# A four-layer graph network on one core: the last norm, scaling and output by halves of the tokens for every graph, and a weight of 0.25 for 0.5 in the planner's order

## The chip, the core and the metric

The kernel runs on one core of a Trainium2 chip. A core has TensorE (PE, matrix products; PEld is its loading of the stationary operand), VectorE (DVE), ScalarE (ACT), GpSimd (POOL) and SyncE (SP), which here issues all DMAs. Each engine works through its own instructions in the order in which the program holds them and waits on semaphores for the others. The metric is the device time of one launch in microseconds.

## The reference

There are 32 graphs of N = 512 nodes with D = 256 features, each with an adjacency matrix of 512 x 512, all float32. Four layers follow each other, each with a residual and a layer norm without weights:

```python
def _layernorm(x, eps=1e-5): return (x - mean(x)) / sqrt(var(x) + eps)      # over the features
# layer 0: h = (1+eps)*x + adj@x;  f = relu(h@W1 + b1)@W2 + b2             (256 -> 512 -> 256)
# layer 1: h = adj@(x@W.T + b);    f = h where h > 0 else alpha*h
# layer 2: h = layer_norm(x)*gamma + beta;  f = x + relu((adj@h)@W_rel + b_rel + h@W_root)
# layer 3: h = (eps*x + adj@x)@W1 + b1;  f = silu(rmsnorm(h)*w)@W2 + b2    (256 -> 1024 -> 256)
# after each: x = _layernorm(x + f(x, adj))
```

Graphs don't depend on each other.

## The kernel before, in words

The tokens of a graph lie on 128 partitions, four to a partition (NC = 4 chunks); a "half" is two of the four chunks (HC = 2). Every matrix product is split into two by two blocks and made from seven block products, m1 to m7 (`seven`, line 651), with sums of the left and right blocks made ahead on DVE (`left_sums`, `right_sums`, `dense_sums`). Of a layer's products, `aggregate` is the one with the adjacency, `dense_feat` gives a result with features on partitions, and `dense_add` (line 850) adds its result into the residual: its `take` and `put` are DVE additions from PSUM, and it calls `done(j)` when half j of the tokens is complete. The three PSUM banks that `seven` uses are each filled anew after their additions were made.

The code does not issue instructions as it runs. It records operations (class `Op`) with the tiles that they read and write, and the class `Plan` then puts all of them, of all graphs, in one order, with prices of its own for each engine. At most FLIGHT = 5 graphs are under way at once; tiles come from pools (36 rooms for whole tensors, 11 small ones, 8 PSUM banks), and the planner picks which. Where an operation can run on ACT or DVE, it also picks the engine. An operation's rank is its graph's number times `period`, plus a need (`needs`, line 324): the matmul work of its graph that stands before the first matmul that depends on it, less the way there. For all but matmuls, the need is raised by `near` times the work between the operation and the next matmul that it feeds (capped at 20), so that a higher `near` lets an operation far from a matmul yield more:

```python
return [t if "tensor" in op.ways else t + near * b for op, t, b in zip(self.ops, need, between)]
...
rule = min(RULES, key=lambda rule: self.order(*rule)[0])   # (period, pace, last, near)
```

`last` is the period used for the last three graphs. Of the rules in RULES, the one whose order is the shortest by the planner's own prices is used. Where a two-operand DVE operation would hold up a power on POOL that is just about to start, the planner lets DVE pause; a pause is filled with `memset`s of a tile named `pause` (line 1197).

All instructions of the plan carry line 298 in the profile, and all DMAs of the plan line 316, so they are told apart by tiles: `room` is a whole tensor, `few` a small one, `ps` a PSUM bank, `A` and `L_gnn_W` are weights and their sums, `scrap` is the unused output of ACT's sums.

A layer norm is the class `Norm` (line 896). `half(h)` sums the values and their squared distances from the mean on ACT, per chunk, as soon as half h is complete. Then, in the graphs 0 to 30 after layer 3, `scales` makes the four chunks' scales at once: a `tensor_scalar` on DVE (128x4) and a power of -1/2 on POOL (128x4); `scaled` multiplies out the shift on DVE and applies scale and shift to the four chunks, on ACT or DVE (`put`); and one DMA of 512 KB stores the graph. Only the last graph uses `finish(h, ...)`, which does the same for two chunks: a 128x2 `tensor_scalar`, a 128x2 power, a 128x2 multiplication, two chunks scaled, one DMA of 256 KB. In graph 0 and graph 31 the class `NormOnVector` makes the sums on DVE instead.

SP issues, for each graph and in the order of the plan: the adjacency in four parts and x, the diagonals of two block sums out to memory and back, the layer-2 transposes as 16 small copies from room to room, a line with layer 3's scales out and back to all partitions, and the store.

Of the kernel before, what the change touches and what calls it, by code (L numbers as in the profile page):

```python
# [16 lines left out]
LN_EPS = 1e-5  # L17
# [74 lines left out]

RULES = [(42, 2, 10, 0.5), (42, 2, 16, 0.5)]


class Pool:
# [122 lines left out]
class Plan:  # L221
# [126 lines left out]
    def best(self):  # L348


        rule = min(RULES, key=lambda rule: self.order(*rule)[0])
        return self.order(*rule)[1]
# [109 lines left out]
def tile_gnn_stack(ctx: ExitStack, tc: tile.TileContext, a: dict, out: bass.AP):  # L462
# [26 lines left out]
    B, N, D = a["x"].shape  # L489
# [15 lines left out]
    plan = Plan(nc, FLIGHT)  # L505
# [9 lines left out]
    def alone():  # L515

        return plan.graph in (0, B - 1)
# [19 lines left out]
    def mm(o, lhsT, rhs, first, last):  # L537
        kw = dict(start=first, stop=last, skip_group_check=True)
        way = "tensor", "matmul", matmul_time(rhs.shape[-1]), (lhsT, rhs), kw
        plan.do(o, way, ordered=o.room)  # L540
# [4 lines left out]
    def act(o, x, func, **kw):  # L545
        plan.do(o, scalar(func, span(o), x, **kw))
# [7 lines left out]
    def add(o, x, y):  # L554
        plan.do(o, vector("tensor_add", span(o), x, y))
# [4 lines left out]
    def mul(o, x, y):  # L560
        plan.do(o, vector("tensor_mul", span(o), x, y))
# [20 lines left out]
    def room(*shape):  # L582
        return Part(Room(rooms)).shaped(*shape)

    def short(*shape):
        return Part(Room(rooms, whole=False)).shaped(*shape)
# [4 lines left out]
    def bank(*shape):  # L591
        return Part(Room(banks)).shaped(*shape)
# [4 lines left out]
    def half(t, h):  # L597
        return t[:, h * HC : (h + 1) * HC]
# [52 lines left out]
    def seven(x, y, z, product, take, put):  # L651


        product("m1", x, True)
        take(x, 0, 0)
        product("m5", z, True)
        take(z, 1, 1)
        product("m2", y, True)
        put(y, 0, 0, True)
        product("m6", x, False)  # L660
        take(x, 0, 1)
        product("m3", z, False)
        put(z, 0, 1, True)
        product("m7", x, False)
        put(x, 1, 1, True)
        product("m4", x, False)
        put(x, 1, 0, False)
# [29 lines left out]
    def blocks_of(*halves):  # L697

        return (W[:, :, i * P : (i + 1) * P] for i in range(2) for W in halves)
# [67 lines left out]
    def aggregate(x, adjacency):  # L767

        aT = room(DC, N)
        blocks = [  # L770
            x[:, j * HC : (j + 1) * HC, k * P : (k + 1) * P] for j in range(2) for k in range(2)
        ]
        t = room(4, HC, P)
        right = right_sums(*blocks, [t[:, i] for i in range(3)], t[:, 3])

        def product(m, ps, first):
            for k in range(HC):
                mm(ps, right[m][:, k, :], adjacency.left[m][:, k, :], first and k == 0, k == HC - 1)

        def block(i, k):  # L780
            return aT[:, k, i * TH : (i + 1) * TH]

        def take(ps, i, k):
            copy(block(i, k), ps)

        def put(ps, i, k, more):
            if more:
                add(block(i, k), ps, block(i, k))
            else:
                take(ps, i, k)  # L790

        seven(*(bank(TH) for _ in range(3)), product, take, put)
        return aT
# [13 lines left out]
    def dense_feat(aT, left, bias, hT, done):  # L807


        n = hT.n // 2  # L810
        t = room(3, TH)
        blocks = [aT[:, k, j * TH : (j + 1) * TH] for k in range(2) for j in range(2)]
        right = right_sums(*blocks, [t[:, i, :] for i in range(3)], blocks[1])
        for f0 in range(0, n, 2):

            def product(m, ps, first):
                for i in range(2):
                    w = left[m][:, (f0 + i) * P : (f0 + i + 1) * P]
                    mm(ps[:, i, :], w, right[m], first and i == 0, True)

            def block(i, j):
                return hT.pair(i * n + f0)[:, :, j * TH : (j + 1) * TH]

            def take(ps, i, j):
                for e in range(2):
                    f = i * n + f0 + e
                    act(block(i, j)[:, e], ps[:, e, :], AF.Identity, bias=bias[:, f : f + 1])

            def put(ps, i, j, more):
                if more:  # L830
                    add(block(i, j), ps, block(i, j))
                else:
                    take(ps, i, j)
                if i != j:
                    done(i * n + f0)

            seven(*(bank(2, TH) for _ in range(3)), product, take, put)
# [12 lines left out]
    def dense_add(x, right, left, done):  # L850


        def block(i, j):
            return x[:, j * HC : (j + 1) * HC, i * P : (i + 1) * P]

        def product(m, ps, first):
            n = len(right[m])
            for k in range(n):
                for i in range(HC):
                    mm(  # L860
                        ps[:, i, :], right[m][k][:, i * P : (i + 1) * P], left[m][:, k, :],
                        first and i == 0 and k == 0, k == n - 1,
                    )

        def take(ps, i, j):
            add(block(i, j), ps, block(i, j))

        def put(ps, i, j, more):
            take(ps, i, j)
            if i == 1:  # L870
                done(j)

        seven(*(bank(HC, P) for _ in range(3)), product, take, put)
# [123 lines left out]
    def everywhere(sums, ops):  # L997

        if alone():
            few = small(2, NC)  # L1000
            ve, power = few[:, 0, :], few[:, 1, :]
            by_token(ve, sums, *ops)
            inv_sqrt(power, ve)
            o = bank(N)
            for c in range(NC):
                flip(o[:, c * P : (c + 1) * P], power[:, c : c + 1].spread(P, P))
        else:
            few, turned = small(2, Q), small(Q)[0:Q]
            ve, square = few[0:Q, 0, 0 : N // Q], few[0:Q, 1, :]
            ts(ve, sums, *ops)  # L1010
            inv_sqrt(square[:, 0 : N // Q], ve)
            plan.do(turned, vector("transpose", Q, square))
            o, line = short(N), next(lines)
            name = line.tensor.name
            plan.move(line.rearrange("(m i) -> m i", i=Q), turned[0 : N // Q], N / 256, into=name)
            plan.move(o, line.partition_broadcast(P), P * N / 256, late=0.8, outof=[name])
        return o

    def plus_row(x, r):

        for h in range(2):
            add(half(x, h), half(x, h), r.unsqueeze(1).to_broadcast([P, HC, D]))
# [77 lines left out]
    def layer3(x, adjacency, b):  # L1100

        aT = aggregate(x, adjacency)
        plus_row(x, b2_3)
        hT, acc = Wide(FC3), short(N)

        def squares(f):
            sq = room(2, N)
            act(sq, hT.pair(f), AF.Square)
            if f == 0:
                add(acc, sq[:, 0, :], sq[:, 1, :])  # L1110
            else:
                add(acc, acc, sq[:, 0, :])
                add(acc, acc, sq[:, 1, :])

        dense_feat(aT, A1_3, b1_3, hT, squares)
        pr = everywhere(column_sums(acc), (1.0 / HID3, RMS_EPS, ALU.mult, ALU.add))
        right = {}
        for q in range(0, FH, 2):
            for f in (q, q + 1, FH + q, FH + q + 1):
                mul(hT.chunk(f), hT.chunk(f), pr)  # L1120
                act(hT.chunk(f), hT.chunk(f), AF.Silu, scale=w_3[:, f : f + 1])
            for m, t in dense_sums([hT.pair(q)], [hT.pair(FH + q)]).items():
                right[m] = right.get(m, []) + t
        norm = (NormOnVector if alone() else Norm)(x)
        place = out[b].rearrange("(p c) d -> p c d", c=NC)
        if b < B - 1:
            dense_add(x, right, A2_3, norm.half)
            norm.scales((1.0, LN_EPS))
            y = norm.scaled()
            plan.move(place, y, N * D / 256, into=f"out{b}")  # L1130
        else:

            def done(h):
                norm.half(h)
                norm.finish(h, 1.0, LN_EPS, half(place, h))

            dense_add(x, right, A2_3, done)

# [11 lines left out]
    x = load_x(0)  # L1152
# [12 lines left out]
    x = layer0(x, adjacency)  # L1165
# [9 lines left out]
    h = layer1(x, adjacency)  # L1175
# [9 lines left out]
    A2_3 = weight_sums("A2_3", *blocks_of(W2_3[:, 0:FH], W2_3[:, FH:]))  # L1185
    layer3(layer2(*h, adjacency), adjacency, 0)
    for b in range(1, B):
        plan.graph = b
        x, adjacency = load_x(b), Adjacency(b)
        h = layer1(layer0(x, adjacency), adjacency)  # L1190
# [45 lines left out]
```

## Time and profile before

| | |
|---|---|
| median of 3 runs | 2318.61 us (2318.61 to 2320.24) |
| profiled execution, its own time | 2319.3 us |
| its span, first to last instruction | 2317.5 us, at a granted TensorE clock of 0.999 |
| PE matmul / weight load busy | 2295.5 us (99%) / 2089.9 us (90%) |
| DVE / ACT / POOL busy | 2120.0 us (91%) / 1642.6 us (71%) / 256.9 us (11%) |
| chain that ended last | PE 89%, DVE 7%, ACT 2% |
| stores of 512 KB, 256 KB | 31 of 3.2 us, 2 of 2.4 us to landing (median) |

One record of a 128x256 or 128x128 float32 matmul is half of an instruction: each such product has two records. The span is the time that the profiler saw instructions; the execution's own time has 1.8 us more around it. A share of busy time is an average over start, steady state and end, so the stretches have to be read one by one. In the table of stretches, a count in parentheses is the number of instructions that are in the stretch.

### The profile page before, as it was taken

Reading aid. Unit: us, or ns where it says so; the run is one execution under the profiler, and the core shown is the slowest. Engines: PE = TensorE matmul, PEld = TensorE weight load, DVE = VectorE, ACT = ScalarE, POOL = GpSimd, SP = SyncE. Lnnn points to the kernel's source line nnn. Section 1 sums busy time; section 2 is a strip of 40 time slices with the busy share of each in tenths; the row PEclk is TensorE's granted clock in tenths of the full one; section 3 lists DMA queues with packets and bytes.
Section 4 is the critical chain, followed back from the end, with each engine's and each line's share of the span. In section 5 each row is a group of like instructions: output and inputs, shape, how many; then the busy total and the mean of one; then the engine's idle time right before and its main releaser. Section 6 shows DMA issues by size and latency. Waiting matters only on the chain.

```text
span 2317.5 us, 41158 instructions
## 1 busy us (share of the span) xinstructions
PE 2295.5 (99%) x14002; PEld 2089.9 (90%) x14002; DVE 2120.0 (91%) x5428; ACT 1642.6 (71%) x4444; POOL 256.9 (11%) x167
## 2 busy tenths in 40 slices
PE   9999999999999999999999999999999999999998
PEld 7889899999999999999999999999999999998988
DVE  8989999999899999999999999989999899989897
ACT  4676677776776776777767776767677677676776
POOL 0000001101101101011011111010110101101110
PEclk9999999999999999999999999999999999999999
DMA  7001222112221122211222211222112222201101
GB/s 241 21 18 19 62 58 60 24 55 62 58 60 28 54 59 65 55 43 41 56 65 57 60 25 56 61 58 59 38 46 58 65 55 52 78 13 24 55 15 42
DMA packets 223746, 122.83 MB, mean 53 GB/s; under 512 B 142896, under 2 KB 194352, under 8 KB 223536
## 3 DMA queue, kind: packets, MB, share of 16 engines
q1 hardware_dynamic: 223536, 120.20, 19.1%
q8 instruction: 111, 1.82, 0.3%
q14 instruction: 99, 0.81, 0.1%
HBM read 78.92 MB, written 24.97 MB: 45 GB/s over the span
## 4 chain that ended last, share of the span: by engine, by line
PE 89%; DVE 7%; ACT 2%; DMA 1%; issue 1%; SPq 0%; POOL 0%; ACTq 0%; DVEq 0%
PE ps L298 89%; DVE room L298 6%; ACT room L298 1%; ACT scrap L298 1%; DVE few L298 1%; DMA room<-in_x_dram 1%; DMA L_gnn_W<-in_L_gnn_W_dram 0%; DMA room<-in_adj_dram 0%; DMA L_gnn_b<-in_L_gnn_b_dram 0%; DMA diagonal<-room 0%; SPq L316 0%; ACT L298 0%; DVE A L298 0%; DVE L_gnn_W_root L298 0%; POOL few L298 0%
## 5 line engine op out<-in xcount | busy, mean ns | idle before, releaser
L298 PE MATMUL ps<-room,room 128*128 128x256 f32 x3584 | 930.9, 381 | 5.7 <-DVE room L298 3.2
L298 DVE TENSOR_TENSOR room<-room,room 128x512 f32<-128x512 f32 (+1 forms) x1360 | 773.0, 590 | 5.4 <-ACT room L298 2.8
L298 DVE TENSOR_TENSOR room<-ps,room 128x256 f32<-128x256 f32 (+1 forms) x1344 | 605.6, 469 | 143.7 <-PE ps L298 136.4
L298 PEld LDWEIGHTS ps<-room,room 128*128 128x128 f32 x3584 | 617.3, 191 | 70.3 <-DVE room L298 7.1
L298 PE MATMUL ps<-L_gnn_W,room 128*128 128x128 f32 (+1 forms) x3584 | 544.3, 290 | 1.9 <-DVE room L298 1.0
L298 PEld LDWEIGHTS ps<-L_gnn_W,room 128*128 128x128 f32 x3584 | 505.6, 191 | 33.7 <-ACT room L298 1.9
L298 PEld LDWEIGHTS ps<-A,room 128*128 128x128 f32 x3072 | 460.5, 191 | 47.3 <-DVE room L298 14.1
L298 PE MATMUL ps<-A,room 128*128 128x128 f32 x3072 | 486.9, 276 | 0.9 <-DVE room L298 0.7
L298 POOL TENSOR_TENSOR few<-few,mhalf 128x4 f32<-128x4 f32 (+2 forms) x161 | 256.2, 1598 | 2054.5 <-DVE few L298 1883.1
L298 ACT ACTIVATE room<-room,few 128x256 f32<-128x256 f32 x627 | 335.0, 596 | 159.9 <-DVE few L298 159.7
L298 PE MATMUL ps<-room,L_gnn_W 128*128 128x256 f32 x1536 | 416.4, 380 | 0.6 <-DVE room L298 0.5
L298 ACT ACTIVATE room<-ps,L_gnn_b_c 128x256 f32<-128x256 f32 x768 | 311.0, 476 | 122.3 <-PE ps L298 117.9
L298 DVE TENSOR_TENSOR room<-room 128x256 f32<-128x256 f32 (+1 forms) x640 | 308.7, 492 | 13.9 <-ACT room L298 8.2
L298 PE MATMUL ps<-room,A 128*128 128x256 f32 x1152 | 320.0, 380 | 1.1 <-ACT room L298 0.8
L298 ACT ACTIVATE room<-room 128x1024 f32<-128x1024 f32 (+2 forms) x260 | 240.8, 939 | 87.3 <-DVE room L298 84.4
L298 PEld LDWEIGHTS ps<-room,L_gnn_W 128*128 128x128 f32 x1536 | 274.5, 191 | 30.1 <-DVE room L298 1.9
L298 ACT ACTIVATE room<-ps 128x256 f32<-128x256 f32 (+1 forms) x513 | 180.1, 373 | 153.3 <-PE ps L298 153.1
L298 ACT ACTIVATE scrap<-room,few 128x256 f32<-128x256 f32 x504 | 250.7, 499 | 39.0 <-DVE few L298 38.3
L298 ACT ACTIVATE scrap<-room 128x256 f32<-128x256 f32 x504 | 206.7, 411 | 88.3 <-DVE room L298 79.8
L298 PEld LDWEIGHTS ps<-room,A 128*128 128x128 f32 x1152 | 202.8, 191 | 22.8 <-ACT room L298 2.0
L298 ACT ACTIVATE room<-room,L_gnn_rms_weight_c 128x512 f32<-128x512 f32 x256 | 173.2, 712 | 13.1 <-DVE room L298 11.0
L298 DVE TENSOR_TENSOR room<-room,loop 128x256 f32<-128x256 f32 x256 | 101.1, 411 | 2.9 <-DMA diagonal<-room 1.8
(57 smaller groups left out, 1110.6 us busy)
## 6 DMA issues: line engine op xcount, KB each, us to landing
room<-in_adj_dram SPq DMA_DIRECT2D x128, 256.0 KB, 5.0
room<-in_x_dram SPq DMA_DIRECT2D x31, 512.0 KB, 5.9
out_dram<-room SPq DMA_DIRECT2D x31, 512.0 KB, 3.2
room<-room SPq DMA_DIRECT2D x480, 32.0 KB, 2.0
diagonal<-room SPq DMA_DIRECT2D x62, 128.0 KB, 1.8
room<-in_adj_dram SPq DMA_DIRECT2D x124, 64.0 KB, 1.9
room<-diagonal SPq DMA_DIRECT2D x62, 128.0 KB, 2.2
room<-line SPq DMA_DIRECT2D x30, 256.0 KB, 3.3
```

The source lines that it names most:

```text
L298: getattr(getattr(self.nc, engine), method)(to, *(put(x) for x in args), **kw)
```

## The change

Every graph now uses the path that only the last one had: when half j of the last product is complete, `done` sums that half, and `finish` makes its two scales, scales its two chunks and stores them. The planner has one rule in place of two, with `near` at 0.25 in place of 0.5.

```diff
-RULES = [(42, 2, 10, 0.5), (42, 2, 16, 0.5)]
+RULES = [(42, 2, 10, 0.25)]
...
         norm = (NormOnVector if alone() else Norm)(x)
         place = out[b].rearrange("(p c) d -> p c d", c=NC)
-        if b < B - 1:
-            dense_add(x, right, A2_3, norm.half)
-            norm.scales((1.0, LN_EPS))
-            y = norm.scaled()
-            plan.move(place, y, N * D / 256, into=f"out{b}")
-        else:
-
-            def done(h):
-                norm.half(h)
-                norm.finish(h, 1.0, LN_EPS, half(place, h))
-
-            dense_add(x, right, A2_3, done)
+
+        def done(h):
+            norm.half(h)
+            norm.finish(h, 1.0, LN_EPS, half(place, h))
+
+        dense_add(x, right, A2_3, done)
```

Since all operations are ordered together, both edits can move any instruction of any engine.

## The prediction

> **What bounds the kernel now.** I read the page first: span, then the share of each engine.
>
> ```profile
> span 2317.5 us, 41158 instructions
> ...
> PE 2295.5 (99%) x14002; PEld 2089.9 (90%) x14002; DVE 2120.0 (91%) x5428; ACT 1642.6 (71%) x4444; POOL 256.9 (11%) x167
> ```
>
> PE has no matmul under way for 2317.5 - 2295.5 = 22 us. Where those lie is read from the table of stretches (columns: stretch, length, then busy us of PE, PEld, DVE, ACT, POOL, the clock, DMA share, GB/s):
>
> ```profile
> 0.00:103.00 103.00, 94.98 (x503) 81.72 (x504) 94.72 (x266) 53.87 (x154) 4.95 (x10) 1.00 0.47 145
> 103.00:277.00 174.00, 171.52 (x1029) 154.37 (x1029) 158.57 (x408) 120.10 (x306) 14.69 (x12) 1.00 0.14 32
> 277.00:1966.00 1689.00, 1688.84 (x10333) 1542.48 (x10332) 1553.16 (x3949) 1221.78 (x3331) 197.66 (x120) 1.00 0.20 52
> 1966.00:2309.00 343.00, 340.13 (x2142) 311.37 (x2140) 310.74 (x797) 242.70 (x647) 37.83 (x25) 1.00 0.13 36
> 2309.00:2317.50 8.50, 0.00 (x0) 0.00 (x0) 2.86 (x13) 4.14 (x11) 1.72 (x3) 0.66 0.47 185
> ```
>
> The idle time is 8.0 us at the start, 2.5 us while the flight of graphs fills, 0.2 us in 1689 us of steady work, 2.9 us while it runs out, and 8.5 us after the last matmul. PE bounds nearly all of it.
>
> "Busy" can hide matmuls that are spaced out, so I count. The groups by form give, per graph, 212 records of 128x256 and 224 of 128x128. In the timeline, a run of four of the first from 101.43 lasts 1.03 us, (1.03 - 0.38)/3 = 0.216 us each after the first (a lone one takes 0.38); a run of twenty of the second from 2297.74 lasts 2.40, (2.40 - 0.28)/19 = 0.112. The floor is 212 x 0.216 + 224 x 0.112 = 70.9 us; the load of x recurs every 71.2 us. About 0.3 us a graph is lost, about 7 us over some 24 steady graphs. One part shows at one place in the timeline (start, length, engine, work):
>
> ```profile
> 1066.06 0.14 DVE L298 TENSOR_TENSOR few<-few 128x4 f32<-128x4 f32 x1
> ...
> 1066.14 0.41 DVE L298 TENSOR_TENSOR room<-ps,room 128x256 f32<-128x256 f32 x1
> ...
> 1066.59 0.52 PEld L298 LDWEIGHTS ps<-A,room 128*128 128x128 f32 x4 [0.33 <-DVE room L298]
> ```
>
> In layer 2's last product the weight load waits for a DVE addition; the matmul comes 0.53 us after the one before, where 0.43 is its pace: 0.1 us, once a graph. DVE is late there because it is full for most of a graph:
>
> ```profile
> 992.60:1032.60 40.00, 40.00 (x239) 36.08 (x237) 39.71 (x109) 32.02 (x90) 5.38 (x4) 1.00 0.10 26
> 1032.60:1046.60 14.00, 14.00 (x78) 12.66 (x77) 8.72 (x16) 8.39 (x17) 0.00 (x0) 1.00 0.63 172
> 1046.60:1063.80 17.20, 17.20 (x126) 16.33 (x124) 16.98 (x44) 11.05 (x37) 2.89 (x1) 1.00 0.06 17
> ```
>
> Of one graph's 71.2 us DVE rests 5.8, nearly all of it in one stretch of 14 us. Outside that stretch, added DVE work has no room of its own: it is paid out of how far DVE runs ahead of PE.
>
> **What the skill says.** The Trainium skill, Perfetto Trace Analysis, "Identifying the Most-Contended Engine", says that matmul busy time does not tell the distance to the limit and that weight-load busy time does; the trace agrees (99% against 90%), hence the count of records above. The same skill, SBUF — State Buffer, "SBUF: two separate sides", says that GpSimd and VectorE take a shared port pair exclusively, and a blocked one waits for a whole instruction. The trace does not show it: beside the 2.89 us power on POOL from 1058.68, DVE additions with two SBUF operands take 0.40 to 0.41 us, their usual time. So I price no blocking for the added powers. DMA: Bandwidth & Descriptors, "Latency and other measured facts", puts a fixed cost of about 2 us on a DMA, so a half isn't half as long; the trace agrees (median 3.2 us to landing for 512 KB out, 2.4 for 256 KB).
>
> **The change, part by part.** *Rules.* The instruction order of the kernel before is that of rule (42, 2, 10, 0.5) alone; dropping the second rule changes nothing. *near from 0.5 to 0.25* adds no operation and reorders. *Halves* add, in each of 31 graphs, one TENSOR_SCALAR and one TENSOR_TENSOR of 128x2 on DVE, one power on POOL, one DMA issue on SP. The engines' orders also hold 157 pauses (memsets on DVE ahead of an operation that must let a power through) where 72 were: in 24 graphs there are 5 where there was 1, before a layer-3 product `mul`, because the PSUM addition that stood between the layer-2 scale and it has moved. Prices, from the groups of instructions (count, then busy us and mean ns of one, then the idle time before):
>
> ```profile
> L298 POOL TENSOR_TENSOR few<-few,mhalf 128x4 f32<-128x4 f32 x97 | 116.7, 1204 | 716.6 <-DVE few L298 635.1 <-DVE pause L1197 48.9 <-ACT scrap L298 29.7
> ...
> L1197 DVE MEMSET pause<- 128x48 f32 x72 | 7.1, 98 | 2.5
> ...
> L298 POOL TENSOR_TENSOR few<-few,mhalf 128x2 f32<-128x2 f32 x2 | 1.4, 696 | 2.6 <-DVE few L298 2.6
> ```
>
> POOL: 2 x 0.70 for 1.20, +0.2 us a graph on an engine 89% idle: free. SP: one more issue, 0.54 us; each DMA waits for its half's scaling, and behind it in SP's queue stand layer 2's transposes and the loads of the next graph (4 of adj, one of x). The first half's store stands ahead of the transposes, the second in the old place just ahead of the loads, which are used a graph later; I price it at 0, covered by that lead. If the early store were held up, the transposes and then layer 2's last product would be late. ACT does the same scalings, 4 a graph. DVE: two small ops at a pace of about 0.07 (a pair of such ops takes 0.22, one 0.16) and 4 memsets of 0.098: 0.14 + 0.39 = 0.53 us a graph, and the memsets stand in the full stretch.
>
> *Steady state.* In both orders PE's matmuls repeat graph after graph; beside the matmuls of other work, few operations of a graph have moved by over 3 us. At the place of the 0.1 us stall, the work on PE between layer 2's second product and the late matmul was two 128x256 and eight 128x128 matmuls (2 x 0.43 + 8 x 0.224 = 2.65 us); now three and eight, 3.08 us, for a DVE sequence that is a transpose shorter. The stall should go: -0.1. A new tight place is layer 0's first dense product on its first difference: four wide and four narrow matmuls, 2.6 us, cover an addition, two 128x512 transposes and a subtraction, 0.34 + 2 x 0.63 + 0.41 plus 0.26 for three hand-overs = 2.27 us; 0.35 us is left at best where 1.4 us stood, and less if DVE arrives late. What the 0.53 us cost PE isn't shown before. Bounds: -0.3 a graph (all waiting gone) and +0.53 (no cover). I take -0.05, since the stall goes and some of the lead is spent: 24 x -0.05 = -1.2 us.
>
> *Start and run-out.* All engines' orders are the same up to ACT's operation at 101.5 us; PE's first difference is its 257th matmul, at 103.25. So the 8.0 us stays. From there to 277 and from 1966 the orders differ; 5.4 us of idle is at stake and is dealt anew: I take 0, bounds -3 and +4.
>
> *Tail.* The chain of waits ends not in graph 31 but in graph 30: four scalings of graph 29, its own totals, its scale, a power, then scalings.
>
> ```profile
> 2306.95 2.07 ACT room L298 x4
> ...
> 2310.29 1.02 POOL few L298
> ```
>
> By halves, graph 29's scalings come before PE ends, and half of graph 30's. The power is 0.70 for 1.02, one or two 0.49 us scalings leave the end. Graph 31's own chain, unchanged, is next late; its last scaling would end about 1 us before the old end. Last stores are 2 x 256 KB for 512 + 256. I take -1.2, bounds -2 and 0.
>
> **Sum** against the profiled execution (2319.3; span 2317.5 and 1.8 around it): -1.2 - 1.2 = -2.4, so 2316.9; the median shown is 2318.61, 0.7 lower, hence 2316.2. A measurement of this kernel tells about 0.2% from no change, 4.6 us.
>
> **Rivals.** *No change to speak of, 2316.2*: for it, the shared order and PE's floor. Chance 0.55. *Faster, 2311*: half of the 0.3 us a graph (24 x -0.15 = -3.6), -2 at run-in and run-out, -1.7 in the tail: -7.3. For it: the stall has cover now, and halves free rooms sooner; against: most of the loss isn't at one place that the change touches. Chance 0.27. *Slower, 2330 at its full price*: DVE becomes the bound in its full stretch. The 5 memsets before the layer-3 product, and the two small operations, go straight to PE's next waiting matmul: 24 x 0.53 = +12.7 beside the tail's -1.2. Half of it gives 2324. It decides once PE's cover behind the pause is used up; from 0.24 us a graph on (+5.8) it shows as slower. For it: DVE at 39.71 of 40 us; against: the reordering moved covers too. Chance 0.18, a third of it above 2327. That the edit does nothing is excluded by the orders.
>
> **How the numbers follow.** The likeliest case alone spans 2314 to 2323. The range goes on to both others: 2309, where a fifth of the faster case is left out, and 2327; that leaves out about 0.05 + 0.06.
>
> **What would show it.** Right: PE's idle time in 277 to 1966 stays under 2 us, loads of x recur within 0.1 us of 71.2, the weight-load wait on the layer-2 addition is gone, the last stretch is 7 to 8 us, memsets 157. Wrong: PE waiting on DVE in every graph behind the 5 memsets or at layer 0's dense product, a period of 71.4 or more, or SP's loads landing late.

## The result, and the profile after

The changed kernel takes 2342.5 us (median of 4 runs, 2340.91 to 2342.85) beside 2319.43 us for the kernel before in the same session: a ratio of 1.0098, interval 1.0086 to 1.011, 23 us slower. It lies outside the predicted range of 2309 to 2327. The profiled span is 2340.7 us.

The head of the page, with the shares by engine, hides it:

```profile
span 2340.7 us, 41411 instructions
...
PE 2307.0 (99%) x14002; PEld 2087.4 (89%) x14002; DVE 2142.8 (92%) x5574; ACT 1650.4 (71%) x4445; POOL 261.2 (11%) x198
```

The shares have moved by a point at most. The chain that ended last, by engine, has moved from PE 89%, DVE 7% to:

```profile
DVE 53%; PE 36%; issue 5%; ACT 4%; DMA 1%; DVEq 0%; SPq 0%; ACTq 0%; POOLq 0%; POOL 0%
```

The table of stretches (columns as in the prediction) says where:

```profile
0.00:103.00 103.00, 94.74 (x502) 81.51 (x502) 94.10 (x264) 53.23 (x152) 4.37 (x9) 1.00 0.47 145
103.00:277.00 174.00, 172.48 (x1052) 158.23 (x1052) 162.19 (x419) 123.96 (x322) 20.90 (x14) 1.00 0.14 32
277.00:1966.00 1689.00, 1677.07 (x10192) 1516.23 (x10191) 1551.88 (x4022) 1211.37 (x3277) 192.59 (x140) 1.00 0.19 51
1966.00:2332.00 366.00, 362.30 (x2260) 331.20 (x2260) 331.77 (x859) 258.04 (x687) 41.58 (x33) 1.00 0.14 39
2332.00:2340.70 8.70, 0.37 (x4) 0.18 (x2) 2.84 (x14) 3.81 (x10) 1.81 (x3) 0.72 0.36 136
```

PE's idle time in 277 to 1966 is 1689.00 - 1677.07 = 11.9 us, where it was 0.2; the other stretches are within 1 us of before. Idle time is not all. I add, for every PE record, its distance from the one before less the pace of its kind (0.2165 us for 128x256, which the prediction rounds to 0.216, and 0.112 for 128x128). This pacing loss was 16.8, 5.0 and 5.9 us before (up to 280, 280 to 1950, after 1950) and is now 13.6, 30.6 and 7.0. So steady work loses 25.6 us more, the start 3.2 less and the run-out 1.1 more. The mean period of a graph is 72.3 us, where it was 71.2.

The list of waits in 300 to 1950 (engine waiting, its releaser: us in total, times, longest) names the places:

```profile
PEld ps L298 <- DVE room L298: 31.0, 69, 0.9
...
DVE few L298 <- POOL few L298: 18.6, 23, 0.8
...
PE ps L298 <- DVE room L298: 11.9, 23, 0.5
PEld ps L298 <- ACT room L298: 11.4, 47, 0.3
```

The third line is new, with one wait in each of 23 graphs; before, no such wait was in this window, and the first line stood at 11.9 us. The fourth is new too, but for one wait of 0.3 us: two weight loads a graph now wait for ACT. The timeline shows the place, the same in every graph, about 72.3 us apart:

```profile
1034.50 1.30 DVE L298 STREAM_TRANSPOSE room<-room 128x512 f32<-128x512 f32 x2
1034.61 1.03 PE L298 MATMUL ps<-room,A 128*128 128x256 f32 x4
...
1035.71 0.38 DVE L298 TENSOR_TENSOR room<-room 128x256 f32<-128x256 f32 x1
...
1036.15 0.70 PE L298 MATMUL ps<-room,L_gnn_W 128*128 128x256 f32 x2 [0.52 <-DVE room L298]
```

Two transposes, a subtraction, then layer 0's first dense product on the difference: the "new tight place" of the prediction. The matmul comes 0.68 us later than PE's pace would have it. In this graph (981.2 to 1053.8) PE records are late by 1.47 us in all, if each that is late by over 0.03 us is counted: 0.78 at this product, 0.40 around the two weight loads that wait for ACT, 0.29 elsewhere. A graph of the kernel before has 0.39. The pauses are the other thing to see, in DVE's timeline (start, length, work):

```profile
1015.97 0.15 DVE L298 TENSOR_SCALAR few<-few 128x4 f32<-128x4 f32 x1
1016.07 0.80 DVE L1191 MEMSET pause<- 128x48 f32 x5
1016.78 0.64 DVE L298 TENSOR_TENSOR room<-room,room 128x512 f32<-128x512 f32 x1
```

Five memsets of 98 ns each hold DVE from 1016.07 until the next operation starts at 1016.78, 0.71 us: they start about 0.175 us apart. In the kernel before, the one memset at this place holds DVE for 0.03 us:

```profile
1008.86 0.10 DVE L1197 MEMSET pause<- 128x48 f32 x1
1008.89 0.63 DVE L298 TENSOR_TENSOR room<-room,room 128x512 f32<-128x512 f32 x1
```

### The profile page after: what moved, and what is told of

It reads as the page before. It is cut to its first block, busy times and chain, and to the rows that moved or that the text cites. A ratio compares the mean times of both kernels' runs of the same rounds, so it can differ in the third digit from the quotient of the medians.

```text
span 2340.7 us, 41411 instructions
## 1 busy us (share of the span) xinstructions
PE 2307.0 (99%) x14002; PEld 2087.4 (89%) x14002; DVE 2142.8 (92%) x5574; ACT 1650.4 (71%) x4445; POOL 261.2 (11%) x198
## 4 chain that ended last, share of the span: by engine, by line
DVE 53%; PE 36%; issue 5%; ACT 4%; DMA 1%; DVEq 0%; SPq 0%; ACTq 0%; POOLq 0%; POOL 0%
DVE room L298 48%; PE ps L298 36%; DVE few L298 5%; ACT scrap L298 3%; DMA room<-in_x_dram 1%; DVE pause L1191 0%; ACT room L298 0%; DMA L_gnn_W<-in_L_gnn_W_dram 0%; DMA room<-in_adj_dram 0%; DMA L_gnn_b_rel<-in_L_gnn_b_rel_dram 0%; DVEq L298 0%; SPq L316 0%; DVE A L298 0%; DVE L_gnn_W L298 0%; POOLq L1226 0%
## 5 line engine op out<-in xcount | busy, mean ns | idle before, releaser
L298 PE MATMUL ps<-room,room 128*128 128x256 f32 x3584 | 917.8, 382 | 6.5 <-DVE room L298 3.4
L298 PEld LDWEIGHTS ps<-A,room 128*128 128x128 f32 x3072 | 455.6, 191 | 43.3 <-DVE room L298 12.0
L298 POOL TENSOR_TENSOR few<-few,mhalf 128x2 f32<-128x2 f32 (+3 forms) x192 | 260.5, 1362 | 2074.3 <-DVE few L298 1682.6
L298 PE MATMUL ps<-A,room 128*128 128x128 f32 x3072 | 481.1, 276 | 0.8 <-DVE room L298 0.7
L298 ACT ACTIVATE room<-room,L_gnn_rms_weight_c 128x512 f32<-128x512 f32 x256 | 178.2, 713 | 23.0 <-DVE room L298 22.9
```

Source lines behind the costliest of these rows:

```text
L298: getattr(getattr(self.nc, engine), method)(to, *(put(x) for x in args), **kw)
```

## The experiments

Medians in us and ratios to the kernel before, with 95% intervals. "Added" is the difference of medians to the kernel before measured in the same session (2319.21 to 2319.80). Experiments without pauses replace the loop of memsets by `pass`; the order of all else stays.

**e1: `near` alone.** In the kernel before:

```diff
-RULES = [(42, 2, 10, 0.5), (42, 2, 16, 0.5)]
+RULES = [(42, 2, 10, 0.25)]
```

> The kernel before with the one rule (42, 2, 10, 0.25): no halves. Its order holds 4 memsets ahead of layer 3's product in 25 graphs, where before has 1. A, the memsets in DVE's full stretch decide: in the kernel after, 5 memsets hold DVE 0.72 us a graph where 1 held it 0.03; 4 should hold it about 0.55, so +0.5 x 24 = +12, 2331 us. B, near moves layer 0's subtraction behind the two transposes and that alone decides: as slow as after, 2340. C, the halves' own operations and DVE's wait for the half's power (0.81 us a graph) decide: no change, 2319.

2326.93, 1.0034 [1.0021, 1.0047]: added 7.7, which lies between the expected cases. The steady period is 71.4 and the steady loss 9.7 (5.0 before), the loss after 1950 12.8 (5.9 before). The layer-0 wait isn't there.

**e2: halves alone.** The changed kernel with its `near` back at 0.5:

```diff
-RULES = [(42, 2, 10, 0.25)]
+RULES = [(42, 2, 10, 0.5)]
```

> The kernel after with the rule (42, 2, 10, 0.5) of before: halves, but near as before. Its order has 1 memset ahead of layer 3's product as before and 2 ahead of a column sum's addition in 24 graphs. A: the 2 memsets cost about 0.2 us and the two small pairs of operations 0.25 + 0.2 us of DVE: half of it uncovered, +5, 2324 us; at most +0.65 x 24 = +16. B: no change, 2319. C: nearly all of the loss, 2337 to 2342.

2338.18, 1.0082 [1.0067, 1.0097]: added 19.0. That is the number of case C, but not for its reason: the steady loss is 8.4 only, and the loss after 1950 is 20.9. Two PE waits of its run-out in the timeline:

```profile
2088.59 1.20 PE L298 MATMUL ps<-A,room 128*128 128x128 f32 x8 [3.82 <-DVE room L298]
...
2295.74 0.70 PE L298 MATMUL ps<-room,L_gnn_W 128*128 128x256 f32 x2 [2.23 <-DVE room L298]
```

Behind the first of them the granted TensorE clock is lower for some 7 us (the clock is the number ahead of the last two), while it is 1.00 at this place in the kernels before and after:

```profile
2088.00:2092.00 4.00, 2.90 (x16) 2.67 (x16) 1.98 (x7) 2.05 (x7) 0.70 (x1) 0.70 0.39 135
2092.00:2096.00 4.00, 3.23 (x11) 2.58 (x11) 3.84 (x7) 3.46 (x7) 0.00 (x0) 0.50 0.50 141
```

With 0.95 from 2096 to 2100, this is worth at most about 3.4 us of the 15 that this run-out loses more than before (an estimate from the three clocks). So the effects don't add up: each edit alone gives an order of its own, and the layer-0 stall belongs to the joint order only.

**e3: the changed kernel without pauses.**

```diff
             if op.pause and op.way == "vector":
-                for _ in range(round(op.pause / 0.11)):
-                    nc.vector.memset(pause, 0.0)
+                pass
```

> The kernel after, every instruction in its order, without the 157 pause memsets. A: 0.72 us of DVE a graph go, the period falls from 72.3 to about 71.6: 2342 - 17 = 2325 us. B: 2340. C: 2340. If powers on POOL need the pauses, they are held up and the time rises.

2330.86, 1.005 [1.0035, 1.0065]: added 11.65 where the changed kernel adds 23.1. The memsets are thus half of the loss, 11.4 us. That is less than A expected: of 24 x 0.68 us that they hold DVE, PE pays two thirds. It pays at the weight loads that wait for ACT, which are nearly gone, and the wait at the layer-0 place stays as it was:

```profile
PE ps L298 <- DVE room L298: 11.5, 24, 0.5
...
PEld ps L298 <- ACT room L298: 0.6, 2, 0.5
```

**e4: five memsets in the order of before.**

```diff
-                for _ in range(round(op.pause / 0.11)):
+                n = round(op.pause / 0.11)
+                for _ in range(5 if n == 1 else n):
                     nc.vector.memset(pause, 0.0)
```

> The kernel before, every instruction in its order, with 5 memsets wherever it has 1 (ahead of layer 3's product in 23 graphs, and in a few other places). A: +0.69 us of DVE in the full stretch a graph, at 23 graphs +16 at full price: 2335 us; if the lead over PE covers half, 2327. B and C: 2319 to 2321.

2337.7, 1.0081 [1.0064, 1.0098]: added 18.5. Five memsets hold DVE for 0.72 us here where one held it for 0.03; the run has 108 DVE instructions more, so 27 places with four more each, and 27 x 0.69 = 18.6. PE pays where a weight load waits for ACT, which is behind DVE (list of waits, 300 to 1950; 0.3 us in one wait before):

```profile
PEld ps L298 <- ACT room L298: 22.7, 89, 0.5
```

So DVE time put into the full stretch costs its whole price in the order of before, and about two thirds of it in the changed one (e3).

**e5 and e6: the subtraction ahead of the two transposes.** On the changed kernel, DVE's order alone is edited, with pauses (e5) and without (e6):

```diff
...
-        for op in plan.best():
+        for op in sooner(plan.best(), plan.ops, plan.early, plan.flips):
...
```

`sooner` takes layer 0's subtraction and puts it ahead of the two 128x512 transposes that stand before it.

> The kernel after with one DVE instruction a graph moved: layer 0's first subtraction for the first dense product stands ahead of the two 128x512 transposes instead of behind them; all else, pauses too, in its order. B', that place is what holds PE (0.68 us a graph in after, 0.66 without pauses): the stall goes, 24 x 0.66 = -16: 2326 us. A', DVE as a whole is behind in its full stretch and the place is only where it shows: the wait reappears at the next matmul that DVE feeds, 2338 to 2342 us.

> The same move, and none of the 157 memsets. B': the two causes add up, 2331 - 16 = 2315 us, a little below the kernel before. A': 2327 to 2331 us.

e5: 2339.25, 1.0085 [1.0071, 1.0099], 3 us below the changed kernel; e6: 2328.81, 1.0042 [1.003, 1.0055], 2 us below e3. The subtraction is in time now, and the matmul behind it waits for what was put back. In e6:

```profile
960.22 0.67 PE L299 MATMUL ps<-room,A 128*128 128x256 f32 x2 [0.43 <-DVE room L299]
```

DVE is late as a whole at this point, not with one operation.

**e7: no wait for POOL in the halves.** The shift is multiplied from the power's input instead of its result (so the shift's values are other ones), and DVE needn't wait for POOL.

```diff
             mul(shift, self.less[:, mine], rstd)
+            op, less = plan.ops[-1], self.less[:, mine]
+            issue = lambda: nc.vector.tensor_mul(shift.place(), less.place(), ve.place())
+            op.ways = {"vector": (op.ways["vector"][0], issue)}
```

> The kernel after, but each half's shift in the last norm is multiplied from the value ahead of the power instead of the power, so that DVE does not wait for POOL there (0.81 us a graph in after); the shift is wrong by that, all else in its order. C, that wait costs PE: up to 24 x 0.8 = -19, 2323 us. A' and B': it lies where DVE then waits for PE anyway, no change, 2340 to 2342 us.

2340.88, 1.0095 [1.0081, 1.0109]: no gain to speak of. The new wait of 0.81 us a graph (18.6 us in the list above) is hidden: when it goes, DVE's waits for PE in the same window grow by as much, from 87.1 to 105.1 us.

**e8: the kernel before without pauses** (the edit of e3).

> The kernel before without its 72 memsets. One memset a graph holds DVE 0.03 us there: 24 x 0.03 = 0.7 us, so 2317.5 to 2319.5 us, no change. If powers on POOL need the pauses: slower.

2317.29, 0.9992 [0.9983, 1.0]. Without pauses the kernel before is no slower.

**e9: the halves' small operations on POOL**, in the changed kernel without pauses. `on_pool` issues the operation recorded last on POOL:

```diff
...
             ts(ve, self.squares[:, mine], m / self.n, plus, ALU.mult, ALU.add)
+            on_pool()
             inv_sqrt(rstd, ve)
             mul(shift, self.less[:, mine], rstd)
+            on_pool()
...
```

> The kernel after without memsets, and with the four small operations of the last norm's halves (two scales ahead of the power, two shifts) issued on POOL instead of DVE, at their places in the order. A', DVE's full stretch is the bound: in after these operations and their extra spacing hold DVE about 0.5 us a graph; without them the period falls from 71.95 to about 71.5: 2331 - 24 x 0.45 = 2320 us. If the reordering alone makes DVE late, whatever it has to do: 2330 us. If POOL's slower small operations hold up the stores or DVE's port: over 2331.

2330.04, 1.0044 [1.003, 1.0057], 1 us below e3: a miss for A', and the number of the second case, in which the order alone makes DVE late. The wait at the layer-0 place stays (11.2 us in 23 waits). In the run of DVE operations that is shown at e13, the changed kernel has two more operations of 128x2 than the kernel before and two fewer of 128x4.

**e10: the shift's multiplication on POOL**, in the kernel before without pauses:

```diff
...
             mul(shift, self.less, s)
+            on_pool()
...
```

> The kernel before without memsets, with the five shift multiplications a graph (128x4, 0.07 us each on DVE) issued on POOL behind the power. A': DVE's full stretch is 0.35 us shorter, but PE loses only about 0.2 us a graph there: 24 x -0.1 to -0.2, 2313 to 2316 us against 2319.4. If the step from POOL to ACT gets longer, PE waits at layer 1's and layer 3's first products: 2320 or more.

2326.39, 1.003 [1.0019, 1.0042]: 9 us above e8, a miss for A' and the number of the second case. A multiplication takes 0.38 us on POOL where it took 0.15 on DVE. ACT's scalings wait 151.3 us for it in 300 to 1950 (142.0 in e8, for DVE). PE's weight loads wait 19.7 us for a releaser that the profile doesn't name (5.2 in e8). That ACT is the link between the two is not shown.

**e11 and e12: each edit alone, without pauses** (e1 and e2 with the edit of e3).

> near at 0.25 alone, without memsets. A': 0.54 us of memsets a graph go; with only them between it and before, 2319 us or less, its run-out being 6 us worse: 2319 to 2323 us. If near's order itself makes DVE late: 2325 us or more.

> Halves alone, without memsets. In its run-out PE loses 19 us where before loses 5.5; in the steady state 8 where before loses 5. If the memsets (0.31 us a graph) make that steady loss: 2338 - 3 = 2335 us. If memsets in the run-out are its loss: 2325 us.

e11: 2320.42, 1.0004 [0.9995, 1.0012], as expected; e12: 2332.86, 1.006 [1.0046, 1.0074], nearer to the first of its two cases. Without pauses the four orders give 2317.3 (before), 2320.4 (`near`), 2332.9 (halves) and 2330.9 (both). Lost in steady work and after 1950: 5.7 and 4.0, 2.2 and 14.6, 7.2 and 19.9, 21.3 and 5.5 (the profiled execution of e12 took 2336.63 us, 3.8 above its median, and has a stretch at half the clock as e2 has). Each edit alone loses mostly in the run-out, both together in steady work.

**e13 and e14: more matmuls ahead of the waiting one.** By now the theory was a balance. DVE has an unbroken run in each graph: it begins with a layer-3 addition from PSUM after a wait of 1.8 us for PE, and reaches layer 0's first subtraction without a rest worth the name. In the table of stretches, from that start to the subtraction's end, of the kernel before and then of the changed one (length, then busy us of PE, PEld, DVE):

```profile
973.78:1027.10 53.32, 53.32 (x342) 49.01 (x341) 52.73 (x140) 39.21 (x114) 8.27 (x5) 1.00 0.07 22
```

```profile
981.30:1036.09 54.79, 54.33 (x344) 49.17 (x342) 53.78 (x145) 39.81 (x114) 7.59 (x5) 1.00 0.11 34
```

Before, the run takes 53.32 us, and the first matmul that needs the subtraction starts 54.7 us after its beginning, with 1.4 us to spare:

```profile
1028.47 0.59 PE L298 MATMUL ps<-room,L_gnn_W 128*128 128x256 f32 x2
```

Now the run takes 54.79 us, and the matmuls that PE has ahead of the same consumer take 53.5 us at their pace (145 records x 0.216 + 198 x 0.112; the expectations of e13 and e14 count one record less): 1.3 us short. The matmul starts at 1036.15, 1.3 us late by this count: 0.68 of it is its own wait, the rest was lost by PE within the run, 0.4 of it at the weight loads that wait for ACT. DVE has 1.47 us more, nearly all of it 0.68 of memsets and two 128x256 operations (0.334 each) that stood behind this point. PE has 0.86 us less: two 128x256 matmul operations, of two records each at 0.216, that stood ahead now follow. If that is the cause, matmuls moved forward cure it and nothing on DVE need change:

```diff
...
-        for op in plan.best():
+        for op in later(plan.best(), plan.ops, plan.early, plan.late):
...
```

In 24 graphs, `later` takes the next three operations of PE that belong to other work (two wide, one narrow: 2 x 0.432 + 0.224 = 1.09 us) and puts them ahead of the waiting product. e13 keeps the pauses, e14 drops them.

> The kernel after, memsets too, with one change on PE in 24 graphs: the three matmuls that follow layer 0's waiting dense matmul and are not of that product go ahead of it (two 128x256 and one 128x128, 1.08 us). In after DVE needs 54.8 us from the start of its unbroken run to the subtraction that this matmul reads, and PE has 53.3 us of matmuls for it; in before 53.3 and 54.1. D, this balance decides: with 54.4 us of matmuls 0.4 us are missing, about 1.0 us less: 24 x 0.9 = -20, 2321 us. E, DVE is behind at all its consumers and the wait moves on: 2337 to 2341 us.

> The same order on PE, without the memsets. D: DVE needs 54.1 us, PE has 54.4: no wait there, 2331 - 16 = 2315 us, below the kernel before by its better run-in. E: 2327 to 2331 us.

e13: 2328.31, 1.0037 [1.0023, 1.0051], 14 us below the changed kernel, but 7 above what D expected. e14: 2317.97, 0.9991 [0.9982, 0.9999]: the whole loss is gone, and the wait at the layer-0 place with it. In e14's table of stretches the steady stretch is nearly back where it was before, at 0.9 us of idle time (the pacing loss in it is 7.1 us, 5.0 before and 21.3 in e3; the run-in is 2.9 better than before):

```profile
277.00:1966.00 1689.00, 1688.09 (x10315) 1538.87 (x10314) 1562.27 (x3960) 1221.77 (x3316) 204.15 (x142) 1.00 0.20 52
```

DVE's busy time in it is higher than in the changed kernel (1562.27 for 1551.88): more work is done in the same stretch. Between e13 and e14 the memsets alone cost 10.3 us, paid at weight loads that wait for ACT (16.2 us in 59 waits with them, 5.1 in 14 without). e13's layer-0 wait is gone as well, so the memsets are what it has left. No kernel tried is faster than the one before by more than 0.1%: e8 and e14 lie 2.2 and 1.7 us below it, with intervals that end at 1.0 and 0.9999.

## Why the prediction was wrong, point by point

- **The step that failed is *steady state*, "-0.05 a graph".** It is about +1.1 (25.6 us of pacing loss over some 24 graphs): by place, 0.78 more at layer 0's first dense product, 0.40 more at the weight loads that wait for ACT, 0.10 less elsewhere. The first place was named rightly, with "0.35 us is left at best where 1.4 us stood, and less if DVE arrives late". The sum that gave 0.35 was local: it set the last four DVE operations against the last few matmuls. DVE did arrive late, by the sum of its run since its last real wait. The windows shown for e13 could have been drawn from the kernel before and the two orders: 53.3 us of DVE, plus what the order puts ahead, against 54.4 us of matmuls less what it puts behind. The prediction itself wrote that outside its stretch of rest "added DVE work has no room of its own", and then did not add it up. That this balance makes the layer-0 half of the loss is shown by e14 against e3: PE's order alone differs, and 12.9 us go.
- **The term of the memsets was mis-sized.** The four more memsets were priced at 4 x 0.098 = 0.39 us; five in place of one hold DVE for 0.71 - 0.03 = 0.68, because in a row they start 0.175 us apart; PE pays 11.4 us for them (e3). The small operations were put at 0.14 us in the full stretch. In the run that counts there are no more of them than before, and taking four a graph off DVE gains 1 us without pauses (e9).
- **The third rival was right in kind.** "DVE becomes the bound in its full stretch" was given 0.18 and a full price of +12.7. Its own mechanism, the pauses, is 11.4 us of the 23 (e3). That this is close to its price is in part luck: the memsets hold DVE longer than priced, and PE pays only two thirds of it. Left out was what the reordering does at the same time: about as much again. The rival had weighed it as "the reordering moved covers too" and taken no number.
- **The stall at layer 2's last product** went, as predicted. Its matmuls come 0.46 us after the ones before where 0.53 stood, at a pace of 0.43. The kernel before, then the changed one:

```profile
1066.07 0.60 PE L298 MATMUL ps<-room,room 128*128 128x256 f32 x2
1066.60 0.71 PE L298 MATMUL ps<-A,room 128*128 128x128 f32 x4
```

```profile
1075.19 0.60 PE L298 MATMUL ps<-room,room 128*128 128x256 f32 x2
1075.65 0.71 PE L298 MATMUL ps<-A,room 128*128 128x128 f32 x4
```

- **Start, run-in and run-out**: 8.3 us of idle time for 8.0, 1.5 for 2.5, 3.7 for 2.9. Taken as 0; by pacing it is -3.2 and +1.1, in sum within the bounds. e1 and e2 show that the run-out was nevertheless a real risk, which the bound of +4 put too low: either edit alone loses 7 to 15 us more there.
- **Tail**: -1.2 taken, -0.3 found (PE's last matmul ends 8.3 us before the end of the span, 8.6 before). Its stores are half as large and land in 2.2 us as the median, but the end hardly moved. The last two powers start 2.36 us after the start of the last addition from PSUM (2332.41 to 2334.77), where it was 1.30 (2308.99 to 2310.29): ACT's sums for the half start late, behind a small DVE operation that stands behind graph 31's statistics. No run tests this.
- **POOL and SP** cost nothing that shows, as taken, though the power of a half takes 0.87 us as the mean of 64, not 0.70. Nothing in the list of waits of the steady window waits for a DMA. DVE's wait for POOL was not foreseen; e7 shows that it costs nothing.
- **The shared port** of GpSimd and VectorE (the Trainium skill, SBUF — State Buffer, "SBUF: two separate sides") was priced at nothing, since "the trace does not show it". That looked at DVE alone. On POOL's side the traces do agree with the page, that of the kernel before too: 29 of its powers start while a DVE operation with two SBUF operands runs, and 28 of these take over 10% longer than usual (23 of them, of 128x4, 1.76 us for 1.01); none of the 132 others does. In the changed kernel the pauses keep one such addition away from a power; without them (e3) the same power takes 1.38 us for 1.01. First the changed kernel, then e3:

```profile
943.77 0.80 DVE L1191 MEMSET pause<- 128x48 f32 x5
943.90 1.01 POOL L298 TENSOR_TENSOR few<-few,mhalf 128x4 f32<-128x4 f32 x1 [14.08 <-DVE pause L1191]
944.49 0.64 DVE L298 TENSOR_TENSOR room<-room,room 128x512 f32<-128x512 f32 x1
```

```profile
939.20 0.69 DVE L298 TENSOR_TENSOR room<-room,room 128x512 f32<-128x512 f32 x1
939.37 1.38 POOL L298 TENSOR_TENSOR few<-few,mhalf 128x4 f32<-128x4 f32 x1 [14.22 <-DVE few L298]
```

  DVE's additions of that kind keep their time when they start beside a power (404 ns as the median of 197 of 128x256 in the kernel before, 417 without a power), so the wait that the page states is seen in one direction only. For PE the price of nothing was right: the kernel before takes 2317.29 us without pauses (e8). The pauses thus shorten powers, which buys no time here, and cost 11.4 us in the changed order.
- **PE at 99% busy** before and after agrees with the Trainium skill, Perfetto Trace Analysis, "Identifying the Most-Contended Engine": weight-load busy time fell from 90% to 89% while matmul busy time stayed. Even that is a slight sign, and comes from the longer span alone (2089.9 us before, 2087.4 now); the chain's shares, from PE 89% to DVE 53%, are the clear one.

**What stays open.** Why the run-outs of e1 and e2 are so much worse was not tried; their longest waits are on DVE, and why the granted clock falls in e2 is not shown. Of e1's two parts, the pauses cost about 7 us (e1 against e11) and the order 3 (e11 against e8); which moved operation makes the second was not tried.

## What to carry to other kernels

Where an engine off the bound is full for most of a period, an average of 91% says little. Add up its work from its last real wait to each operation that the bounding engine needs, and set that against the bounding engine's own work ahead of that operation; check each such consumer in the new order, and from the start of the run, not from the nearest instruction. Where the balance is short, it can be mended from either side: less work on the full engine, or more of the bounding engine's other work ahead of the consumer. Fillers, such as pauses, are to be priced by what a row of them holds, not by the duration of one.

## What the runs showed of the hardware

- Memsets of one small tile (128x48), in a row, start 0.175 us apart, with a duration of 98 ns each; a lone one holds DVE for only 0.03 us before the next operation starts.
- A 128x4 power on POOL takes 1.01 us, 1.38 when it starts 0.17 us into a DVE addition of 128x512 with two SBUF operands (e3), and 1.76 in 23 cases of the kernel before. In that kernel every power that is lengthened by over 10%, 28 of 161, starts while such an operation runs. DVE additions show no lengthening beside a power (median 404 ns for 128x256, 417 otherwise).
- A 128x4 multiplication takes 0.38 us on POOL and 0.15 on DVE; moving five of them a graph to POOL cost 9 us (e10 against e8).
- In e2 the granted TensorE clock was 0.70 and 0.50 in the 8 us from 2088, behind a PE wait of 3.82 us.
